# Accumulating DMAs for part of the softmax row sums, and keys loaded in two halves

## The chip, the cores and the metric

The kernel runs on one core of one Trainium2 chip. The metric is the device time of one execution in microseconds. A core has five engines that work side by side, each through its own queue, strictly in order: TensorE (PE, matrix products), VectorE (DVE), ScalarE (ACT), GpSimd (POOL) and SyncE (SP). In this kernel SP issues nearly all DMAs, and GpSimd issues those with an index list. An engine waits at the head of its queue until what its next instruction reads has been written and what it overwrites has been read; everything behind that instruction waits too.

## The reference

Two batches of 1024 tokens with 512 features go through one transformer block: attention with 16 heads of 32 features, then a mixture of experts with 8 experts and a shared one, each followed by an addition of its input and a layer norm. The part that the change touches is the attention:

```python
q = _split(lora_linear(x, Wq, bq, Bq, Aq))
k = _split(lora_linear(x, Wk, bk, Bk, Ak))
v = _split(lora_linear(x, Wv, bv, Bv, Av))
scores = jnp.einsum('bhqd,bhkd->bhqk', q, k) * SCALE
attn = jax.nn.softmax(scores, axis=-1)
out = jnp.einsum('bhqk,bhkd->bhqd', attn, v)
...
return lora_linear(out, Wo, bo, Bo, Ao)
```

All arithmetic is float32, and the kernel keeps that precision by splitting operands into a high and a low part.

## The kernel before

The kernel has three stages. The first projects q, k and v and stores them in HBM. The second, about 157 to 630 us of the profile, is the attention with its output projection. The third is the expert layer.

The attention is cut into 16 units. Unit u takes the group g = u // 2 of four heads of one batch and half u % 2 of its queries (512). A unit has eight steps, one for each block kc of 128 keys, so that step t is unit t // 8, block t % 8; there are NS = 128 steps. In step t:

- `st_step` makes, for each of the four heads, 128 keys by 512 queries of scores (st, line 604) and their exponential on ScalarE (line 613). Two heads share one tile pt of 128 x 2 x 512 floats, so a step writes two tiles, called pair 0 and pair 1. The tiles come from a pool of PTB = 13 buffers; a buffer is free again once every reader of its tile is done.
- `s1_step` runs LEAD = 12 steps ahead: four score blocks a step with queries on the partitions (s, line 183), whose row maxima VectorE takes (mt, line 191). They go through three PSUM banks. At the end of a unit `finish_max` transposes the maxima (mp) and stores them by DMA as two further rows of the queries, so that st comes out with the maximum already taken off.
- `av_step(t - 1)` multiplies the last step's exponentials with the values (av, line 634), summed over the unit's eight steps in one PSUM bank.
- `add_step` sums the exponentials of a unit's blocks (line 623): the tiles of block 0 serve as the sums, and those of blocks 1 to 6 are added to them, each with an addition of 128 x 1024 floats for each pair. Block 7 (`DIRECT`) is not added; `finish` reads it by itself. In units 0 to 13 VectorE adds pair 0 of block 1 and pair 1 of block 2 (`ON_DVE`), and GpSimd the rest; for units 14 and 15 `DVE_END` lists what VectorE adds.
- `finish(u)` lets TensorE sum the sums over the keys with a matrix of ones (sm, line 657), in step FIN = 3 of the next unit. Up to unit 13, ScalarE copies the result (rc, line 671) and two small DMAs bring the 2048 denominators onto 128 partitions; `invert(u)` in step REC = 4 takes the reciprocal of 128 x 16 elements (line 681) and spreads it again with five DMAs. From unit RDIR = 14 on VectorE takes the reciprocal of all 128 x 512 at once (line 667).
- `normalize(u)` in step 7 multiplies av with it on VectorE (line 696), copies the high part on ScalarE (698) and subtracts it on VectorE (700).

Beside them SP loads what comes next: `load_k` the keys of the next group, in three DMAs of 512 KB into one of two tiles, in step 0 of an even unit; `load_q` the queries; `load_v` the values; `load_res` blocks of the input x, to which GpSimd adds a bias three steps later (`add_res`, line 709). In units 8 to 10 the first batch's output projection is woven in (`oproj`).

In this stage every engine follows the program's order: the loop over t calls the functions, and what goes between the four heads of a step stands in the lists between[0] to between[3]. No scheduler moves anything. PSUM banks and pt buffers are chosen when the program is built; the chip only waits.

Of the kernel before, what the change touches and what calls it, by code (L numbers as in the profile page):

```python
# [36 lines left out]
OPER = 4  # L37
PTB = 13
OHB = 3
# [14 lines left out]
NO_DIR = (NU - 2,)  # L54
FIN = 3
REC = 4
XTB = 5
ON_DVE = ((1, 0), (2, 1))
EARLY = (1, 0)
OPROJ_AT = (65, 67, 69, 71, 73, 75, 77, 79)  # L60
RES_AT = tuple(8 * i + 6 for i in range(8)) + (70, 78, 86, 94, 98, 102, 106, 110)
RES_ADD = 3
RB = 2
# [4 lines left out]
MPJ, MPP = 0, 2  # L68
RDIR = NU - 2
FINE, NRME = 2, 4  # L70
DVE_END = {
    NU - 2: ((1, 0), (2, 1), (4, 1), (5, 1), (6, 0), (6, 1), (7, 0), (7, 1)),
    NU - 1: ((1, 0), (2, 0), (3, 0), (4, 0), (5, 0), (6, 0), (6, 1)),
# [20 lines left out]
def kernel(  # L94
# [47 lines left out]

    def load_k(g):
        kt = Ks[g % 2]
        for blk, hl in ((0, 0), (1, 1), (2, 0)):
            sp.dma_start(
                out=f(kt[32 * blk : 32 * blk + 32]),
                in_=qk_d[1, g // NG, g % NG, hl].rearrange("(h p) t -> p h t", p=32),
            )
# [435 lines left out]
    with ph2, tc.manual_schedule(engines={mybir.EngineType.PE}):  # L585
# [38 lines left out]

        def early(t, pr):
            return t // 8 not in DVE_END and (t % 8, pr) == EARLY

        def av_step(t):
# [4 lines left out]
            for h in range(4):  # L633
# [7 lines left out]
                )  # L641
            for pr in range(2):
                if not early(t, pr):
                    add_step(t, pr)

        def direct(u):
# [31 lines left out]
        def invert(u):  # L678
            r16 = fin[u]
            rd = dram.tile([4, 512], F32, name=f"rd{u}")  # L680
            dve.reciprocal(r16, r16)
            sp.dma_start(out=rd.rearrange("h (j c) -> (h j) c", c=16), in_=r16)
            rc = ap.tile([P, 512], F32, name=f"rb{u}", tag="rb", bufs=1)
            for h in range(4):
                sp.dma_start(
                    out=rc[32 * h : 32 * h + 32, :],
                    in_=rd[h : h + 1, :].partition_broadcast(32),
                )
            fin[u] = rc
# [56 lines left out]
        for t in range(NS):  # L746
            u, k = t // 8, t % 8
            if k == 0:
                if u % 2 == 0 and 2 <= u and u // 2 + 1 < B * NG:
                    load_k(u // 2 + 1)  # L750
                if u >= 1 and u + 2 < NU:
                    load_q(u + 2)
                if u % 2 and NG <= u // 2 + 1 < B * NG:
                    load_v(u // 2 + 1)
            if t in RES_AT:
                load_res(RES_AT.index(t))
            between = [[], [], [], []]
            if early(t, 0):
                between[2].append(lambda: add_step(t, 0))
            if t + LEAD < NS:  # L760
# [4 lines left out]
            if t:  # L765
                between[1].append(lambda: av_step(t - 1))
                if u and k == (FINE if u == NU - 1 else FIN):
                    between[1].append(lambda: finish(u - 1))
            if u:
                if k == (NRME if u == NU - 1 else 7):  # L770
                    between[0].append(lambda: normalize(u - 1, (0,)))
                    between[1].append(lambda: normalize(u - 1, (1,)))
                    between[2].append(lambda: normalize(u - 1, (2,)))
            if t - RES_ADD in RES_AT:
                between[3].append(lambda: add_res(RES_AT.index(t - RES_ADD)))
            st_step(t, between)
            if k == REC and 1 <= u < NU - 1:
                invert(u - 1)
# [9 lines left out]
            if t - NS >= OPROJ1:  # L788
                next(op10, None)
        av_step(NS - 1)  # L790
        finish(NU - 1)
        normalize(NU - 1, (0,))
# [457 lines left out]
```

## Time and profile before

| What | Value |
|---|---|
| Median of 3 runs | 1080.75 us (1079.41 to 1081.03) |
| Profiled execution, its own time | 1070.33 us |
| Its span, from the first instruction to the last | 1068.6 us |
| Mean granted TensorE clock | 0.991 |
| Busy in the span: PE, DVE, ACT, POOL | 1038.4, 747.8, 530.4, 574.7 us |
| Additions of exponentials on POOL and on DVE | 151 of 2413 ns, 43 of 2132 ns |
| Row maxima on DVE | 512 of 681 ns |
| Keys, queries, median time to landing | 6.9 us, 5.7 us |

The span is that of one execution under the profiler. Busy times are unions of an engine's instructions; TensorE's matrix products overlap and their ends are modelled, so its share tells little about short waits. A group line gives line, engine, operation, output and inputs, shapes and count, then busy time and mean, then the engine's idle time before it and what ended most of it. In answers on waits, "A <- B" is engine A waiting for B's instruction; "issue" means that nothing in the profile explains the wait. PEld is TensorE's load of weights, which comes ahead of the product that uses them. The profiled execution is some 10 us shorter than the median of the runs.

### The profile page before, as it was taken

The numbers are of one execution on the slowest core, as the hardware profiler recorded it, in microseconds if no ns is written. First come the engines' busy times: TensorE is split into PE (matmuls) and PEld (weight loads), VectorE is DVE, ScalarE is ACT, GpSimd is POOL, SyncE is SP. The second block draws the span as 40 slices with busy tenths as digits, with TensorE's granted clock in tenths as the row PEclk, the third lists the DMA queues.
The fourth block names the chain that finished last, engine by engine and source line by source line (L and its number), as shares of the span: only waits on it lengthen the run. The fifth ranks groups of instructions, "written<-read, shape, count | busy, mean of one in ns | idle before, by whom it ended". The sixth has DMA issues, their size and how long they took to land. (4 is left out here: it accounts for less than half of the span.)

```text
span 1068.6 us, 16466 instructions
## 1 busy us (share of the span) xinstructions
PE 1038.4 (97%) x5994; PEld 744.8 (70%) x5994; DVE 747.8 (70%) x1217; ACT 530.4 (50%) x1026; POOL 574.7 (54%) x379
## 2 busy tenths in 40 slices
PE   8999999999999999999999999999999999999996
PEld 6888774444444455554444358889999999999995
DVE  6732787899999987889999785333532457777762
ACT  5422214666666655556666656222322356665552
POOL 5000007888888887768998577000050026776674
PEclk9999998999999999999999999999999999999999
DMA  9866860141414242043520113000073356677731
GB/s 301 278 220 202 256 190 21 42 105 47 110 51 110 71 111 71 15 97 71 120 81 22 52 40 127 23 10 21 21 236 120 108 168 228 241 251 258 251 104 60
DMA packets 77585, 131.24 MB, mean 123 GB/s; under 512 B 14344, under 2 KB 23048, under 8 KB 77504
## 3 DMA queue, kind: packets, MB, share of 16 engines
q1 hardware_dynamic: 73664, 117.59, 37.1%
q0 software_dynamic: 3840, 12.60, 3.2%
q8 instruction: 47, 0.77, 0.3%
q14 instruction: 34, 0.28, 0.1%
HBM read 96.10 MB, written 33.80 MB: 122 GB/s over the span
## 5 line engine op out<-in xcount | busy, mean ns | idle before, releaser
L623 POOL TENSOR_TENSOR pt<-pt,pt 128x1024 f32<-128x1024 f32 x151 | 360.4, 2413 | 206.3 <-ACT pt L613 189.1
L191 DVE TENSOR_REDUCE mt<-s 128x1 f32<-128x512 f32 x512 | 323.8, 681 | 42.5 <-PE s L183 42.4
L613 ACT ACTIVATE pt<-st 128x512 f32<-128x512 f32 x512 | 270.9, 602 | 144.1 <-PE st L604 140.3
L604 PE MATMUL st<-qs,ks 98*128 98x512 f32 x512 | 216.4, 433 | 1.9 <-ACT pt L613 1.2
L183 PE MATMUL s<-ks,qs 96*128 96x512 f32 x512 | 204.1, 406 | 12.8 <-DVE mt L191 11.9
L604 PEld LDWEIGHTS st<-qs,ks 98*128 98x128 f32 x512 | 96.5, 190 | 137.3 <-issue 89.1
L864 PE MATMUL h<-xthe,w13s 128*128 128x256 f32 x704 | 129.9, 284 | 0.0
L183 PEld LDWEIGHTS s<-ks,qs 96*128 96x128 f32 x512 | 97.9, 191 | 41.4 <-DVE mt L191 26.9
L852 POOL TENSOR_TENSOR w2s<-w2r,w2s 128x512 fp32r<-128x512 f32 x42 | 65.9, 1592 | 96.9 <-ACT w2s L851 96.7
L864 PEld LDWEIGHTS h<-xthe,w13s 128*128 128x128 f32 x704 | 110.7, 191 | 0.3
L864 PE MATMUL h<-xtle,w13s 128*128 128x256 f32 x352 | 100.2, 285 | 0.0
L623 DVE TENSOR_TENSOR pt<-pt,pt 128x1024 f32<-128x1024 f32 x43 | 91.4, 2132 | 3.4 <-ACT pt L613 2.9
L634 PE MATMUL av<-pt,vt 128*32 128x512 f32 x512 | 75.0, 605 | 0.0
L634 PE MATMUL av<-pt,x1b 128*32 128x512 f32 x512 | 69.9, 619 | 0.0
L1012 POOL DMA_INDIRECT xd_d<-x1a,slot_i x8 | 8.0, 996 | 112.0 <-DVE slot_i L1009 109.9
L864 PEld LDWEIGHTS h<-xtle,w13s 128*128 128x128 f32 x352 | 67.4, 191 | 0.7
L908 PE MATMUL y<-w2s,hs 128*128 128x512 f32 x260 | 60.9, 390 | 0.0
L908 PEld LDWEIGHTS y<-w2s,hs 128*128 128x128 f32 x260 | 48.2, 188 | 10.2 <-DVE hs L890 0.5
L310 PE MATMUL o<-xl,wh 128*128 128x512 f32 x128 | 50.8, 397 | 0.9 <-POOL xl L296 0.9
L310 PE MATMUL o<-xh,wh 128*128 128x512 f32 x128 | 50.7, 396 | 0.8 <-ACT xh L295 0.8
L325 ACT ACTIVATE oh<-o,bqk_sb 128x512 fp32r<-128x512 f32 x32 | 22.0, 690 | 59.1 <-PE o L310 55.9
L310 PE MATMUL o<-xh,wl 128*128 128x512 f32 x128 | 50.5, 394 | 0.0
(822 smaller groups left out, 1760.2 us busy)
## 6 DMA issues: line engine op xcount, KB each, us to landing
qs<-qkd SPq DMA_DIRECT2D x48, 256.0 KB, 5.7
ks<-qkd SPq DMA_DIRECT2D x24, 512.0 KB, 6.9
x1a<-in_w_dram SPq DMA_DIRECT2D x24, 512.0 KB, 6.1
w2r<-in_w_dram SPq DMA_DIRECT2D x42, 256.0 KB, 2.9
qkd<-oh SPq DMA_DIRECT2D x32, 256.0 KB, 2.5
qkd<-ol SPq DMA_DIRECT2D x32, 256.0 KB, 2.5
x1b<-in_w_dram SPq DMA_DIRECT2D x16, 512.0 KB, 4.9
x1b<-in_wT_dram SPq DMA_DIRECT2D x16, 256.0 KB, 5.2
```

Source lines behind the costliest of these rows:

```text
L183: pe.matmul(s1, Qs[u % 3][0:96, h, qt * P : qt * P + P], Ks[g % 2][0:96, h, kh * 512 : kh * 512 + 512], start=True, stop=True,)
L191: dve.tensor_reduce(mts[u][:, c, kh : kh + 1], s1, AX.X, ALU.max)
L310: pe.matmul(o, lhs, rhs, start=k + i == 0, stop=k + i == KC + 1)
L325: act.activation(oh, o, AF.Identity, bias=bias)
L604: pe.matmul(sb, Ks[g % 2][:, h, kc * P : kc * P + P], Qs[u % 3][:, h, :], start=True, stop=True,)
L613: act.activation(pts[t, h // 2][:, h % 2, :], sb, AF.Exp, scale=SCALE)
L623: eng.tensor_tensor(accs[u, pr], accs[u, pr], pts[t, pr], ALU.add)
L634: pe.matmul(avs[u][32 * h : 32 * h + 32, :], vts[g][:, kc, 32 * h : 32 * h + 32], pts[t, h // 2][:, h % 2, :], start=kc == 0, stop=kc == 7 ...
L852: pool.tensor_tensor(hl[:, 1, :], raw, f(hl[:, 0, :]), ALU.subtract)
L864: pe.matmul(hp[:, j * 256 : j * 256 + 256], lhs, rhs[:, k, :], start=n == 0, stop=n == 11,)
L908: pe.matmul(o, lhs, rhs, start=n == 0, stop=n == 16)
L1012: sc_ = pool.indirect_dma_start(out=xd_d, out_offset=bass.IndirectOffsetOnAxis(ap=slot_i[:, i : i + 1], axis=0), in_=x1[i // 8][:, i % 8, ...
```

## The change

- In units 0 to 13 VectorE no longer adds exponentials. Both tiles of block 1 are added to the tiles of block 2 by DMAs that accumulate, issued by GpSimd in the place of block 2. GpSimd then adds blocks 3 and 4, block 2 (now with block 1 in it), and 5 and 6, each with both pairs: ten additions in a unit, as before. In unit 13 block 6 goes by DMA into block 7 too, and blocks 3, 4, 2 and 5 are added.
- The pool of exponentials gets 14 buffers for 13.
- `finish` moves from step 3 to step 4 of the next unit, `invert` from 4 to 5, `normalize` from step 7 to step 0 of the unit after.
- Unit 13's reciprocal is taken directly (RDIR 13 for 14).
- In unit 14 VectorE adds blocks 1 and 7 of pair 0 and blocks 1 to 7 of pair 1 (nine for eight). Its additions of blocks 1 and 2 are put behind the last maxima, in step 115.
- The keys come in two halves: columns 0 to 511 in step 6 of an odd unit, 512 to 1023 in step 0 of the next unit, two steps later.
- The last two additions of bias to x move to steps 118 and 119.

```diff
-PTB = 13
+PTB = 14
-FIN = 3
-REC = 4
+FIN, FINQ = 4, 1
+REC = 5
+NRM = 0
+K_AT = 6
-ON_DVE = ((1, 0), (2, 1))
-EARLY = (1, 0)
+ON_DVE = ()
+ON_DMA = {NU - 3: (1, 6)}
+ADDS = {0: (0,), 2: (1,), 3: (3,), 4: (4,), 5: (2,), 6: (5,), 7: (6,)}
+ADDS_END = {0: (0,), 2: (1,), 3: (3,), 4: (4,), 5: (2,), 7: (6, 5)}
-RES_ADD = 3
+RES_ADDS = tuple(t + 3 for t in RES_AT[:14]) + (118, 119)
-RDIR = NU - 2
-FINE, NRME = 2, 4
+RDIR = NU - 3
+FINE, NRME = 2, {NU - 2: 7, NU - 1: 4}
 DVE_END = {
-    NU - 2: ((1, 0), (2, 1), (4, 1), (5, 1), (6, 0), (6, 1), (7, 0), (7, 1)),
+    NU - 2: ((1, 0), (7, 0)) + tuple((i, 1) for i in range(1, 8)),
...
-    def load_k(g):
+    def load_k(g, cs=slice(0, 1024)):
         kt = Ks[g % 2]
         for blk, hl in ((0, 0), (1, 1), (2, 0)):
             sp.dma_start(
-                out=f(kt[32 * blk : 32 * blk + 32]),
-                in_=qk_d[1, g // NG, g % NG, hl].rearrange("(h p) t -> p h t", p=32),
+                out=f(kt[32 * blk : 32 * blk + 32, :, cs]),
+                in_=qk_d[1, g // NG, g % NG, hl].rearrange("(h p) t -> p h t", p=32)[:, :, cs],
             )
...
-            for pr in range(2):
-                if not early(t, pr):
+        def adds(t):
+            u, kc = t // 8, t % 8
+            if u in DVE_END:
+                for pr in range(2):
                     add_step(t, pr)
+                return
+            for j, pr in product((ADDS_END if u in ON_DMA else ADDS).get(kc, ()), range(2)):
+                i = u * 8 + j
+                if j in ON_DMA.get(u, (1,)):
+                    pool.dma_start(out=pts[i + 1, pr], in_=pts[i, pr], accum_op=ALU.add)
+                else:
+                    add_step(i, pr)
...
-                    load_k(u // 2 + 1)
+                    load_k(u // 2 + 1, slice(512, 1024))
...
+            if k == K_AT and u % 2 and u // 2 + 2 < B * NG:
+                load_k(u // 2 + 2, slice(0, 512))
...
-            if early(t, 0):
-                between[2].append(lambda: add_step(t, 0))
...
                 between[1].append(lambda: av_step(t - 1))
+                if t == NS - LEAD - 1:
+                    between[3].append(lambda: (adds(t - 2), adds(t - 1)))
+                elif t != NS - LEAD - 2:
+                    between[1].append(lambda: adds(t - 1))
                 if u and k == (FINE if u == NU - 1 else FIN):
-                    between[1].append(lambda: finish(u - 1))
+                    between[1 if u == NU - 1 else FINQ].append(lambda: finish(u - 1))
             if u:
-                if k == (NRME if u == NU - 1 else 7):
-                    between[0].append(lambda: normalize(u - 1, (0,)))
-                    between[1].append(lambda: normalize(u - 1, (1,)))
-                    between[2].append(lambda: normalize(u - 1, (2,)))
-            if t - RES_ADD in RES_AT:
-                between[3].append(lambda: add_res(RES_AT.index(t - RES_ADD)))
+                for v in [u - 2] * (k == NRM and 1 < u < NU - 1) + [u - 1] * (k == NRME.get(u)):
+                    between[0].append(lambda v=v: normalize(v, (0,)))
+                    between[1].append(lambda v=v: normalize(v, (1,)))
+                    between[2].append(lambda v=v: normalize(v, (2,)))
+            if t in RES_ADDS:
+                between[3].append(lambda: add_res(RES_ADDS.index(t)))
             st_step(t, between)
-            if k == REC and 1 <= u < NU - 1:
+            if k == REC and 1 <= u <= RDIR:
                 invert(u - 1)
...
         av_step(NS - 1)
+        adds(NS - 1)
         finish(NU - 1)
```

More of the change, by code (lines that the diff above doesn't have):

```diff
@@ L1 @@
 from contextlib import ExitStack
-from itertools import cycle
+from itertools import cycle, product
 import concourse.bass as bass
@@ L623, in add_step @@
                 eng.tensor_tensor(accs[u, pr], accs[u, pr], pts[t, pr], ALU.add)
-        def early(t, pr):
-            return t // 8 not in DVE_END and (t % 8, pr) == EARLY
         def av_step(t):
@@ L682, in invert @@
             sp.dma_start(out=rd.rearrange("h (j c) -> (h j) c", c=16), in_=r16)
-            rc = ap.tile([P, 512], F32, name=f"rb{u}", tag="rb", bufs=1)
+            rc = ap.tile([P, 512], F32, name=f"rb{u}", tag="rc", bufs=1)
             for h in range(4):
```

## The prediction

> **What bounds the kernel now.** I read the page first: its busy shares and its costliest groups.
>
> ```profile
> span 1068.6 us, 16466 instructions
> PE 1038.4 (97%) x5994; PEld 744.8 (70%) x5994; DVE 747.8 (70%) x1217; ACT 530.4 (50%) x1026; POOL 574.7 (54%) x379
> ...
> L623 POOL TENSOR_TENSOR pt<-pt,pt 128x1024 f32<-128x1024 f32 x151 | 360.4, 2413 | 206.3 <-ACT pt L613 189.1
> L191 DVE TENSOR_REDUCE mt<-s 128x1 f32<-128x512 f32 x512 | 323.8, 681 | 42.5 <-PE s L183 42.4
> ...
> L623 DVE TENSOR_TENSOR pt<-pt,pt 128x1024 f32<-128x1024 f32 x43 | 91.4, 2132 | 3.4 <-ACT pt L613 2.9
> ...
> L1012 POOL DMA_INDIRECT xd_d<-x1a,slot_i x8 | 8.0, 996 | 112.0 <-DVE slot_i L1009 109.9
> ```
>
> TensorE is nearly always busy, but that mean hides stages, and its modelled ends hide short waits. All edits lie in the attention steps, about 157 to 630 us, so next come the busy times by window, one unit of eight steps each (us, TensorE, weight loads, VectorE, ScalarE, GpSimd, clock):
>
> ```profile
> 301.00:329.00 28.00, 27.34 (x147) 13.12 (x146) 25.96 (x41) 17.96 (x37) 24.95 (x12) 1.00 0.18 49
> 422.00:462.00 40.00, 38.65 (x194) 22.05 (x195) 32.67 (x56) 21.43 (x40) 28.43 (x20) 1.00 0.19 50
> ```
>
> In an ordinary unit VectorE is at 93% and GpSimd at 89%; ScalarE has 10 us free. The second row is a unit with output projections in it: there TensorE alone has the work. Who waits for whom in that ordinary unit (us in total, times, longest):
>
> ```profile
> PEld st L604 <- issue: 5.9, 7, 0.8
> ...
> POOL pt L623 <- ACT pt L613: 1.7, 1, 1.7
> PEld s L183 <- DVE mt L191: 1.5, 2, 0.9
> POOL pt L623 <- DVE pt L623: 1.2, 1, 1.2
> ```
>
> So TensorE waits for VectorE twice in a unit. The timeline shows where, in the unit that begins at 273.6 us:
>
> ```profile
> 278.21 1.23 DVE L623 TENSOR_TENSOR pt<-pt,pt 128x1024 f32<-128x1024 f32 x1
> ...
> 280.09 0.19 PEld L183 LDWEIGHTS s<-ks,qs 96*128 96x128 f32 x1 [0.57 <-DVE mt L191]
> ...
> 284.70 3.36 DVE L623 TENSOR_TENSOR pt<-pt,pt 128x1024 f32<-128x1024 f32 x1
> ...
> 288.71 0.19 PEld L183 LDWEIGHTS s<-ks,qs 96*128 96x128 f32 x1 [0.92 <-DVE mt L191]
> ```
>
> Both stalls follow a VectorE addition: the maxima queued behind it are late, the three s banks fill, and TensorE stands. From the first exponential of one step to that of the next, the steps of that unit take 2.95, 3.34, 3.23, 4.80, 4.03, 3.25, 2.99 and 3.24 us, 27.8 together; neighbours agree within 0.1.
>
> **What the Trainium skill says.** "SBUF — State Buffer", section "Who interferes with whom": a VectorE instruction with two SBUF inputs contends with a GpSimd one that reads SBUF, and the later one blocks. The trace agrees: the addition takes 1.23 us while GpSimd waits and 3.36 us beside its additions. "DMA: Bandwidth & Descriptors", section "SWDGE vs HWDGE vs iDMA": accumulation in a DMA is for GpSimd's queue only, which writes the descriptors in software. The kernel before has no such DMA. Its section "Specifications" puts that path's start at about 1 us; the indirect DMAs here are near it, 996 ns.
>
> **The change, part by part, in an ordinary unit.**
>
> VectorE loses 1.23 + 3.36 = 4.59 us, from 25.96 to 21.4 us. The two stalls go. What is TensorE's own time? A step without a stall is 3.02 us; the row sums (sm) add 1.73 (from av at 283.59 to the next st at 286.31 it takes 2.72 us instead of 0.99); the transpose of the maxima adds 0.40 (2.47 instead of 2.07 us for four pairs). Steps 3 to 5 should then take 3 x 3.02 + 1.73 + 0.40 = 11.19 us and take 12.08; step 2 has 0.2 to 0.5 too much. So 1.3 us at most can go, to 26.5 us.
>
> GpSimd now adds pair 1 of step 1, pair 0 of step 2 and both pairs of steps 3 to 6. After the change both pairs of step 1 go by DMA into step 2's tiles, and it adds both pairs of steps 2 to 6: ten again. Ten at 2.36 (two take 4.70 to 4.75) and one residual addition of 1.1 to 1.3 are 24.9 us, as now. New are two DMA issues of d each: 24.9 + 2d. No row has d. Low end: SP's issues take 0.43 to 0.54 us, so 0.4. High end: nothing excludes that reading two operands and writing one costs twice an indirect one, so 2.0. The nearest row, eight scatters of 128 rows, has 996 ns busy, and the eight start 1.3 us apart (778.3 to 787.4). A plain copy reads no index list but has a second operand to read: I take 1.1. Then GpSimd needs 27.1 us, 0.6 more than TensorE and 0.75 less than now. Break-even with 27.85 is d = 1.48.
>
> Does GpSimd's lateness reach TensorE at once? Counted from a unit's start, the DMA can be issued at 11.3 us (av of step 2 must have read the tile), and the last addition ends at 11.3 + 2.2 + 24.9 = 38.4. The row sum needs it in step 4 of the next unit, at 26.5 + 14.2 = 40.7: the move of FIN from 3 to 4 makes that slack of 2.3 us. A lag of 0.6 a unit uses it up in four units. Behind it, exponentials of later steps wait for the same tiles (14 buffers instead of 13; the build gives the tile of step 4 that of step 6 before).
>
> The DMA itself: 512 KB, 3.2 us by the skill's fit ("Anatomy of one DMA — SWDGE (gpsimd) path": 2.0 us plus bytes over 436 GB/s), 4.4 us if the destination's bytes count too; both are estimates. Step 2's sum is added after steps 3 and 4, 9.4 us later, which hides it. Tighter: the build lets the exponential of step 5 reuse the source tile of step 1, 6.7 us after the issue starts. And REC follows FIN by 0.8 us less than now: the denominators' second transfer is issued 1.7 us after the first and landed some 1.7 us before the reciprocal; the long step moves before it. Together I charge 0.3 us a unit; without VectorE's new slack it would be up to 1.
>
> At nothing: normalize moves from step 7 to step 0 of the next unit with the same three instructions (0.69 + 0.59 + 0.68 us), its av buffer is wanted a step later, and VectorE's freed time hides it; uncovered it costs the 0.24 us that step 7 shows now. The keys' halves add three SP issues of 0.43 us per group; a whole load issued at 273.25 landed at 282.5, its first reader came after 288. SP waits for nothing long there; uncovered a late key would cost the 3 us by which it missed. The residual additions moved to steps 118 and 119 fall where GpSimd idles 9.3 us.
>
> The sum against the span of 1068.6:
> - Units 1 to 7 and 11 to 13: seven or so at 1.3 (the first four of each stretch), three at 0.75, less 0.3 each: 9.1 + 2.25 - 3.0 = 8.4 us gained.
> - Units 8 to 10, with projections: waits on VectorE of 1.0, 1.6 and 2.1 us; two thirds, 3.0. GpSimd has 8 to 12 us free there.
> - Unit 0: 4.6 us of such waits, most under a lower clock; 1.0.
> - Units 14 and 15: unit 14's first stall (0.9) goes. But after the last maxima VectorE gets three more additions (1.2 to 2.5 each) and the whole reciprocal of unit 13 (3.36 as for unit 14, instead of 0.25): 6.7 to 10.6 us more, where it idles 6.8 before sm. Taken as 1.9 lost, net 1.0 lost.
>
> 8.4 + 3.0 + 1.0 - 1.0 = 11.4 us. The span becomes 1057 us; the profiled execution took 1070.33, 1.7 more than its span, and would take 1059. The runs' median is 10.4 us above that execution; the shift is carried over: 1080.75 - 11.4 = 1069 us. Nothing after 630 us changes.
>
> **The rivals.**
> - TensorE becomes the only bound (d at most 0.8, no other waits). For it: GpSimd has 2.9 us a unit free. Then 10 x 1.3 + 4.7 + 2 less 1: 18.7 gained, 1062 us. Chance 0.17.
> - The gain is eaten: GpSimd at d = 1.4 to 1.55 takes the whole unit, or the exponential of step 5 waits about 1 us for the DMA. Only units 8 to 10 gain: 1078 to 1083, 1080 us. For it: GpSimd is already at 89%. Against: d is above every indirect DMA seen but the output's (1392). Chance 0.10.
> - Slower: an issue on GpSimd costs over 1.55 us. At d = 2.0 a unit takes 28.9, ten lose 1.05 each, the end loses 2 and units 8 to 10 gain 3: +9.5, 1090 us. From d = 1.55 it decides, in GpSimd's queue between the two stretches of additions. A DMA that lands later than 7 us does the same through the buffers. Chance 0.16.
> - My forecast, 1064 to 1076: chance 0.57.
>
> **How the numbers follow.** 0.2% of the median, 2.2 us, is about what a measurement of this kernel can tell from no change. Faster: 0.17 + 0.57 and a little of the third case, 0.76. Slower: the last case and the rest of the third, 0.17. Same: 0.07. The range leaves out the worse half of the slower case and the tail below: 1058 to 1085; the likeliest one's own is 1064 to 1076.
>
> **What would show it.** No wait of s weights on mt above 0.3 us in units 1 to 7; VectorE near 21.4 us in such a unit; 16 VectorE additions instead of 43; 30 accumulating DMAs whose issue on GpSimd is 0.9 to 1.3 us; units of 26.5 to 27.3 us. Wrong it is if GpSimd is without idle time and units take 27.8 or more, if exponentials wait for a DMA or for GpSimd, or if the last row sums come more than 3 us later after the maxima's end.

## The result and the profile after

The changed kernel takes 1074.3 us (median of 8 runs, 1071.12 to 1076.1); the kernel before, run beside it, 1080.39 us (8 runs, 1078.66 to 1081.8). The ratio is 0.9942, 95% interval 0.9929 to 0.9956: 6.1 us faster. The forecast was 1069 us and 11.4 us gained, range 1058 to 1085, so the time lies in the range and in the forecast's own part of it (1064 to 1076), with half of the gain missing.

The page of the changed kernel, its busy shares and the groups that answer to those shown of before:

```profile
span 1070.8 us, 16471 instructions
PE 1033.8 (97%) x5994; PEld 744.5 (70%) x5994; DVE 697.2 (65%) x1190; ACT 529.2 (49%) x1025; POOL 596.1 (56%) x406
...
L627 POOL TENSOR_TENSOR pt<-pt,pt 128x1024 f32<-128x1024 f32 x148 | 362.0, 2909 | 11.3 <-ACT pt L617 10.8
...
L187 PE MATMUL s<-ks,qs 96*128 96x512 f32 x512 | 200.3, 398 | 5.3 <-DMA qs<-qkd 4.2
...
L655 POOL DMA_DIRECT2D pt<-pt x30 | 27.4, 1078 | 170.5 <-PE st L608 170.5
```

The line of the s products in the kernel before:

```profile
L183 PE MATMUL s<-ks,qs 96*128 96x512 f32 x512 | 204.1, 406 | 12.8 <-DVE mt L191 11.9
```

VectorE lost 50.6 us of work, GpSimd issued 30 accumulating DMAs, and TensorE's s products, which used to wait for maxima (11.9 us), now wait for the queries (4.2 us), whose transfers stand behind the keys' in SyncE's queue. But this span is 2.2 us longer than the one shown of before, although the runs are 6.1 us faster. A second profiled execution of the kernel before, the first of the experiments, has a span of 1078.7 us. With it the spans divide like this (us; a unit lasts from its first exponential to that of the next, and the last two end with the first exponential of the last step):

| Stretch | before, shown | before, second | after |
|---|---|---|---|
| start to unit 0 | 157.1 | 158.0 | 158.4 |
| unit 0 | 32.75 | 31.16 | 25.69 |
| units 1 to 7 | 195.0 | 195.1 | 191.0 |
| units 8 to 10 | 107.6 | 107.6 | 103.6 |
| units 11 to 13 | 83.9 | 84.0 | 81.2 |
| units 14 and 15 | 47.5 | 47.6 | 52.5 |
| last exponentials at | 623.9 | 623.4 | 612.4 |
| from there to the end | 444.7 | 455.3 | 458.3 |

The last exponentials come 11.0 to 11.5 us earlier, but not where the forecast put it: unit 0 gave 5.5 to 7.1, units 1 to 13 gave 10.7 to 10.9, the end took 4.9 back, and the first unit began 0.4 to 1.3 later. The last row, whose code is the same, differs by 10.6 us between the two executions of one and the same kernel.

The windows of three units after the change: an odd one, an even one, and unit 14 (columns as before: us, TensorE, weight loads, VectorE, ScalarE, GpSimd, clock, DMA share, GB/s):

```profile
293.80:320.40 26.60, 26.60 (x147) 13.06 (x145) 21.50 (x38) 17.66 (x36) 25.78 (x14) 1.00 0.39 81
320.40:348.40 28.00, 26.79 (x146) 13.01 (x145) 21.57 (x38) 17.79 (x36) 27.65 (x15) 1.00 0.70 147
560.00:592.10 32.10, 27.10 (x135) 11.07 (x134) 30.63 (x30) 17.87 (x36) 24.53 (x11) 0.95 0.29 72
```

In the odd unit TensorE is busy throughout, and the waits of s on a maximum are gone. In the even unit it stands 1.2 us, with the DMAs busy 70% of the time. The waits of the even unit name what it stands for (mx reduces a unit's maxima to one for each query of each head):

```profile
PEld s L187 <- DVE mx L198: 1.6, 1, 1.6
PE s L187 <- DMA qs<-qkd: 1.2, 1, 1.2
```

Both belong to one and the same s, the first that reads the new keys and queries: its weights' load is put down to mx, the product itself to the queries. That the transfer is what it waited for is shown by the version with x behind the keys below, in which neither wait is left. The DMA issues on SyncE ahead of that wait show the two halves of a key load (ks), the residual block (x1a) and the queries (qs):

```profile
317.79 1.73 SPq L698 DMA_DIRECT2D rb<-rd  x4
319.62 1.32 SPq L150 DMA_DIRECT2D ks<-qkd  x3
320.98 0.43 SPq L718 DMA_DIRECT2D x1a<-in_x_dram  x1
321.51 1.32 SPq L150 DMA_DIRECT2D ks<-qkd  x3
322.88 2.33 SPq L170 DMA_DIRECT2D qs<-qkd  x3
```

"Two steps apart" is 1.9 us here: the early half stands behind the spread reciprocals (rb) in SyncE's queue, and then both halves, x and the queries fill the DMA engines until 332.4; s goes on at 333.81. In the kernel before, the transfers of the same unit filled the engines from 329.5 to 340.2 us, the last part of the queries landed at 341.37, and the first s that reads them ran at 343.30.

Unit 14 on VectorE:

```profile
573.06 5.66 DVE L627 TENSOR_TENSOR pt<-pt,pt 128x1024 f32<-128x1024 f32 x3
578.65 0.27 DVE L209 TENSOR_TENSOR ml<-mp,mh 16x128 fp32r<-16x128 f32 x1
578.85 3.18 DVE L627 TENSOR_TENSOR pt<-pt,pt 128x1024 f32<-128x1024 f32 x1
581.95 3.34 DVE L680 RECIPROCAL rc<-sm 128x512 f32<-128x512 f32 x1
```

Three additions stand ahead of ml, the low part of the last maxima. TensorE's next st needs the PSUM bank that ml reads, so it stands 2.14 us (576.8 to 579.0), runs the 3.4 us from 579.3 at half clock, and step 4 of unit 14 takes 7.7 us instead of the 5.0 of an odd unit. The late reciprocal then delays normalize, and step 7 takes 5.5 us.

### The profile page after: what moved, and what is told of

The parts are those of the page before. It is cut to its first block, busy times and chain, and to the rows that moved or that the text cites. A ratio compares the mean times of both kernels' runs of the same rounds, so it can differ in the third digit from the quotient of the medians.

```text
span 1070.8 us, 16471 instructions
## 1 busy us (share of the span) xinstructions
PE 1033.8 (97%) x5994; PEld 744.5 (70%) x5994; DVE 697.2 (65%) x1190; ACT 529.2 (49%) x1025; POOL 596.1 (56%) x406
## 3 DMA queue, kind: packets, MB, share of 16 engines
q0 software_dynamic: 8160, 28.33, 10.7%
## 5 line engine op out<-in xcount | busy, mean ns | idle before, releaser
L627 POOL TENSOR_TENSOR pt<-pt,pt 128x1024 f32<-128x1024 f32 x148 | 362.0, 2909 | 11.3 <-ACT pt L617 10.8
L608 PE MATMUL st<-qs,ks 98*128 98x512 f32 x512 | 214.1, 428 | 3.3 <-DVE ml L209 2.1
L187 PE MATMUL s<-ks,qs 96*128 96x512 f32 x512 | 200.3, 398 | 5.3 <-DMA qs<-qkd 4.2
L655 POOL DMA_DIRECT2D pt<-pt x30 | 27.4, 1078 | 170.5 <-PE st L608 170.5
L928 PEld LDWEIGHTS y<-w2s,hs 128*128 128x128 f32 x260 | 48.2, 188 | 10.2 <-DVE hs L910 0.5
L314 PE MATMUL o<-xh,wh 128*128 128x512 f32 x128 | 50.6, 395 | 1.7 <-ACT xh L299 1.0
```

Of the source, the lines that this page charges most:

```text
L187: pe.matmul(s1, Qs[u % 3][0:96, h, qt * P : qt * P + P], Ks[g % 2][0:96, h, kh * 512 : kh * 512 + 512], start=True, stop=True,)
L314: pe.matmul(o, lhs, rhs, start=k + i == 0, stop=k + i == KC + 1)
L608: pe.matmul(sb, Ks[g % 2][:, h, kc * P : kc * P + P], Qs[u % 3][:, h, :], start=True, stop=True,)
L627: eng.tensor_tensor(accs[u, pr], accs[u, pr], pts[t, pr], ALU.add)
L655: pool.dma_start(out=pts[i + 1, pr], in_=pts[i, pr], accum_op=ALU.add)
L928: pe.matmul(o, lhs, rhs, start=n == 0, stop=n == 16)
```

## The experiments

All ratios are to the kernel before, run on the same chip.

| Version | us, median | ratio, 95% interval |
|---|---|---|
| kernel before again | 1079.8 | 1.0005 (0.9992 to 1.0018) |
| before, VectorE's additions left out | 1060.08 | 0.9812 (0.9788 to 0.9836) |
| after, VectorE's additions back, no DMAs | 1116.77 | 1.0343 (1.0311 to 1.0374) |
| after, DMAs left out | 1071.09 | 0.9910 (0.9883 to 0.9938) |
| before, accumulating DMAs alone | 1118.27 | 1.0350 (1.0334 to 1.0366) |
| after, x behind the keys | 1071.85 | 0.9917 (0.9889 to 0.9945) |
| after, keys whole | 1075.46 | 0.9941 (0.9920 to 0.9961) |
| after, early half at step 5 | 1084.84 | 1.0049 (1.0031 to 1.0067) |
| after, old end of additions | 1073.32 | 0.9932 (0.9908 to 0.9956) |
| after, early half at step 5 and old end | 1088.84 | 1.0084 (1.0059 to 1.0109) |
| after, ml ahead of additions | 1074.74 | 0.9943 (0.9924 to 0.9963) |
| after, x behind the keys, unit 14 shared anew | 1070.49 | 0.9894 (0.9873 to 0.9914) |

### The kernel before once more

No edit.

> The kernel before once more, for another profiled execution of it. In its profiled execution the expert layer's 16th to 24th gated products take 24.0 us of the trace, in the changed kernel's and in every one of the experiments' so far 30.6 to 38.5 us, with TensorE at half clock for 10 us there; its median is 10 us above that execution. If the stall while the tokens are scattered is part of an ordinary execution of this program too, and the profiled one was a lucky one: this one's profile shows it (32 us or more, half clock for 10 us), and its own time is 1078 to 1082 us. If the change makes the stall: it is missing here again and the profiled time is near 1070 us. The ratio of the times is 1.00 in both cases.

The window from the 21st to the 36th gated product of the expert layer (by their activations), in the execution shown of before:

```profile
762.70:833.80 71.10, 71.10 (x505) 67.07 (x504) 24.66 (x78) 14.71 (x39) 15.65 (x16) 1.00 0.43 138
```

and in this second one:

```profile
762.10:844.00 81.90, 75.96 (x505) 69.22 (x504) 24.56 (x78) 14.72 (x40) 15.62 (x16) 0.94 0.37 120
```

The same instructions take 10.8 us more: TensorE is idle for 5.9 us of the window and at half clock for 10.2 us. The changed kernel's execution takes 82.4 us there, and every other version's profile has half clock for 10.2 or 13.7 us in this stall. So the stall belongs to ordinary executions of both kernels, and the one shown of before was without it: that is the 10 us by which it lay below the median. A second execution of before therefore compares better with after's. Why the weight loads stall there for what the trace calls issue, during the scatter of the tokens, wasn't tried.

### VectorE's additions left out of the kernel before

```diff
                 eng = dve if (kc, pr) in DVE_END.get(u, ON_DVE) else pool
+                if eng is dve and u not in DVE_END:
+                    return
...
-            act.copy(rc, sm)
+            act.activation(rc, sm, AF.Identity, bias=ones32[:, 0:1])
```

> The kernel before with VectorE's two additions a unit left out in units 0 to 13, nothing in their place: those exponentials are missing from the row sums, and 1.0 is added to the sums of units 0 to 13 as they are copied, so that no sum is zero. Theory (VectorE's additions hold back the maxima and nothing else binds): ordinary units fall from 27.85 to 26.5 us, with no wait of s weights on mt in steps 2 and 3; 15 to 18 us in all with units 8 to 10, ratio 0.983 to 0.986. Rival (GpSimd at 89% is next and sets the pace): units stay above 27.3 us, ratio above 0.992.

One of its ordinary units (columns as above):

```profile
290.80:317.50 26.70, 26.70 (x146) 13.02 (x145) 21.49 (x38) 17.87 (x36) 24.80 (x12) 1.00 0.19 52
```

27.85 us became 26.7, unit 0 took 25.68 us, no product of TensorE waits more than 1.0 us in the attention, and no stretch of it runs at half clock. The last exponentials come at 603.0 us, 20.4 us earlier than in the second execution of before, and the runs are 18.8 us faster, somewhat more than the first theory's 15 to 18. Together with the next experiment this shows the prediction's cause: the two additions, by way of the maxima, were what kept TensorE waiting. It is also about the gain that the change could have had with transfers that cost nothing and the old end: after reaches 612.4.

### VectorE's additions back in the changed kernel

```diff
-ON_DVE = ()
+ON_DVE = ((1, 0), (2, 1))
+EARLY = (1, 0)
...
-            if u in DVE_END:
-                for pr in range(2):
+            for pr in range(2):
+                if not early(t, pr):
                     add_step(t, pr)
-                return
+            return
...
+            if early(t, 0):
+                between[2].append(lambda: add_step(t, 0))
```

What follows that return, the accumulating DMAs among it, is no longer reached.

> The changed kernel with VectorE's two additions per ordinary unit put back where the kernel before has them (the pair (1,0) ahead of a maximum's pieces in step 2, the pair (2,1) after it), GpSimd adding the rest and no accumulating DMA at all; every other edit of the change stays (keys in two halves, later reciprocal and normalize, the split of the last additions). My theory, that VectorE's additions delay the maxima: the odd units go from 26.65 us back to 27.5 to 28.0 us, with waits of TensorE's s on a maximum again, and the even ones, where the late keys already cost 1.2 to 1.5 us, to 28 us or a little more; over 11 units that is 8 to 13 us, 1082 to 1088 us, a ratio to the kernel before of 1.002 to 1.008. Rival, that the other edits (the later normalize and reciprocal) made the units shorter and the DMAs did nothing: units stay within 0.3 us of the changed kernel's and the time within 3 us of 1074 us, 0.993 to 0.997.

Far slower than either expectation. Waits of units 2 to 4 on TensorE:

```profile
PE s L188 <- DVE mt L196: 6.9, 6, 1.9
```

The waits on maxima are back, in step 2 and, larger than before, in step 4: 1.9 us against 0.92. Six stretches of half clock (3.4 us each) follow such waits in the attention, a seventh the wait on ml in unit 14 that the changed kernel has too, and ordinary units take 28.1 to 33.8 us. That the sums' products, now a step later than the addition, no longer cover part of the wait is the likely reason why it grew; it is argued, not shown. Shown is that the rest of the change (the later row sums, inversions and normalizations, the halves of the keys and the end's new split) gains nothing by itself: with VectorE's additions it costs 36.6 us.

### The DMAs left out of the changed kernel

```diff
-                    pool.dma_start(out=pts[i + 1, pr], in_=pts[i, pr], accum_op=ALU.add)
+                    if u in ON_DMA:
+                        pool.dma_start(out=pts[i + 1, pr], in_=pts[i, pr], accum_op=ALU.add)
...
-            act.copy(rc, sm)
+            act.activation(rc, sm, AF.Identity, bias=ones32[:, 0:1])
```

> The changed kernel with the accumulating DMAs left out in units 0 to 12, so that block 1 of the exponentials is missing from these units' sums of rows (1.0 is added to each sum in their inversion instead, so the output is another); unit 13 keeps its four. It tells what the DMAs themselves cost. Theory, that they are free, since GpSimd has room and TensorE's own work is the bound: odd units stay at 26.6 to 26.7 us, even ones at 27.9 to 28.4 us since the keys' transfers remain late, 1072 to 1076 us, ratio 0.992 to 0.996. Rival, that their 512 KB per unit crowd the DMA engines and are what makes the keys late: even units fall by 0.7 us or more in step 4, 1067 to 1071 us, ratio 0.988 to 0.991. Rival, that issuing them holds GpSimd's additions by the recorded 2.2 us a unit and through them the sums: the waits of the sums' matmuls get shorter by 1 us or more and units of both kinds shorten.

Odd units from 3 on stay at 26.6 to 26.8 us: for them the DMAs are free. Step 4 of unit 2 falls from 6.73 to 5.21 us, that of unit 12 from 6.44 to 5.93, that of unit 6 hardly (6.45 to 6.33). So their traffic is a part of the keys' lateness and not all of it, and at most a few us in all: the interval overlaps that of the change. The attention ends 2.7 us earlier, and another 2.1 us are saved at the very end of the program, where each accumulating DMA has a price of its own (see the last part of why the prediction was right).

Their issue on GpSimd can be read in the changed kernel's timeline:

```profile
277.93 1.77 POOL L655 DMA_DIRECT2D pt<-pt  x2 [0.35 <-PE st L608]
279.08 24.05 POOL L627 TENSOR_TENSOR pt<-pt,pt 128x1024 f32<-128x1024 f32 x10
...
305.17 1.77 POOL L655 DMA_DIRECT2D pt<-pt  x2 [0.82 <-PE st L608]
```

One record lasts 1.08 us, but the pair is over in 1.15 us, when the first addition starts: each holds the queue 0.57 us. The ten additions follow at 2.35 us as before, although their records grew to 2.9 us, since they overlap. In the changed kernel they end 8.6 to 10.9 us into the next unit. GpSimd then waits for TensorE again: it is not the bound.

### The DMAs alone in the kernel before

```diff
-PTB = 13
+PTB = 14
...
-ON_DVE = ((1, 0), (2, 1))
+ON_DVE = ()
+ADDS = {0: (0,), 2: (2,), 3: (1,), 4: (4,), 5: (5,), 6: (3,), 7: (6,)}
...
+            for j, pr in product(ADDS.get(kc, ()), range(2)):
+                i = u * 8 + j
+                if j == 1:
+                    pool.dma_start(out=pts[i + 2, pr], in_=pts[i, pr], accum_op=ALU.add)
+                else:
+                    add_step(i, pr)
...
-            rc = ap.tile([P, 512], F32, name=f"rb{u}", tag="rb", bufs=1)
+            rc = ap.tile([P, 512], F32, name=f"rb{u}", tag="rc", bufs=1)
```

The 14th buffer and the one buffer that rc and rb share are in the changed kernel too.

> The kernel before with one part of the change alone: VectorE adds nothing in the ordinary units, and GpSimd's queue issues accumulating DMAs that add block 1 into block 3 instead (block 3 is added to the sum late, after block 5, so that the sums can end where they did). Keys come whole, reciprocal, normalize and the last two units' additions stay as they were. If the DMAs' part carries the whole gain and the other parts of the change cost what the odd and even units and unit 14 show (1.2 to 1.5 us in each even unit, 5 us in unit 14): units at 26.7 to 26.9 us, unit 14 at about 27 us, 1060 to 1064 us, ratio 0.981 to 0.985. If the sums now come late because GpSimd is full (10 additions of 2.35 us, the residual's 1.1 us and the issue of 1.15 us are 25.8 of 26.7 us), as I assumed when I moved the reciprocal with the rest: a wait of 1 us or more at the sums' matmuls in step 3 of each unit, units of 27.5 us or more, and 1070 us or more.

The first expectation missed by far, and the second has the time but not the cause: the kernel is 35 us slower, though no sum waits for GpSimd. The DMAs were issued on GpSimd at 264.21 and 264.8. SyncE's issues after that, in which rd stores the small reciprocals and rb can be issued only when rd has landed:

```profile
266.67 0.92 SPq L689 DMA_DIRECT2D rd<-r  x1
271.51 1.73 SPq L692 DMA_DIRECT2D rb<-rd  x4
```

SyncE's wait ahead of rb is put down to rd (3.9 us), not to the shared buffer. The windows between (the last two columns are DMA share and GB/s):

```profile
266.00:268.00 2.00, 2.00 (x13) 0.89 (x13) 1.23 (x3) 0.88 (x3) 2.00 (x2) 1.00 1.12 217
268.00:270.00 2.00, 2.00 (x14) 0.86 (x12) 2.00 (x4) 1.78 (x4) 2.00 (x2) 1.00 1.07 207
```

The accumulating pair fills all DMA engines until 271 (a share above 1 comes from packets that overlap), and a store of 8 KB lands only with its end: 4.84 us from rd to rb, 4.8 to 6.5 in the units up to 13, against 1.6 to 1.7 in most units of before. The store's 128 packets run from 269.25 to 270.97, between those of the pair; in the changed kernel they take 0.2 us (261.97 to 262.17). The Trainium skill says why this may be ("DMA: Bandwidth & Descriptors", section "Issuing engines are not separate DMA queues"): transfers of all issuing engines run on the same 16 DMA engines and interleave there. The trace agrees: those 1.7 us are spent side by side with the pair. What the delay holds up is on VectorE (four units, from 246 to 400 us):

```profile
DVE mt L191 <- PE s L183: 37.4, 40, 2.3
DVE av L703 <- DMA rb<-rd: 11.2, 4, 3.5
```

normalize waits 2 to 3.5 us for rb at the head of VectorE's queue, with the maxima behind it; TensorE follows, and half clock follows that in 11 places. In the changed kernel the pair is issued a step earlier (in flight from 252 to 258 in that unit), rd goes out at 261.13 when it has landed, and rb 1.46 us later; and normalize has another step to spare. The change's own order of DMAs with the old places of sum and normalize wasn't tried. GpSimd's additions end 8.6 to 10.9 us into the next unit in the changed kernel, and the old row sum begins 10.5 us into a unit in the version without VectorE's additions, so it might have fitted in most units; that is not shown.

### Keys: the residual block behind them

```diff
-RES_AT = tuple(8 * i + 6 for i in range(8)) + (70, 78, 86, 94, 98, 102, 106, 110)
-RES_ADDS = tuple(t + 3 for t in RES_AT[:14]) + (118, 119)
+RES_AT = tuple(8 * i + 8 for i in range(8)) + (72, 80, 88, 96, 98, 102, 106, 110)
+RES_ADDS = tuple(t + 4 for t in RES_AT[:13]) + (105, 118, 119)
```

> The changed kernel with the loads of the residual blocks (256 KB each) moved from step 6 of a unit to step 0 of the next, behind keys and queries in SyncE's queue, so that they no longer stand between the two halves of a key load; their additions move along by as much. If the even units' longer step 4 (6.4 to 6.7 us against 5.03) comes from keys that land late behind that block: step 4 of units 2, 6 and 12 falls by 0.7 to 1.2 us, 3 to 5 us in all, 1069 to 1071.5 us, ratio 0.989 to 0.992. If the block hardly matters and the second half of the keys is late because it is issued at step 0 with less lead over its reader than before: step 4 stays at 6.4 us or more and the time within 2 us of 1074 us.

Step 4 of units 2, 6 and 12 falls to 5.01, 5.12 and 5.03 us; TensorE waits for no transfer in units 1 to 7, and all ordinary units take 26.5 to 26.8 us. The attention ends at 606.4 us, 6.0 earlier than after the change. The runs show 2.4 us of it, with overlapping intervals; the rest of the program took 460.7 us in the profiled execution against 458.3, with half clock for 13.7 us in the expert layer's stall against 10.2. That the 256 KB between the halves, ahead of the queries, made them late is shown by the steps; its worth in time is known only to a few us.

### Keys: whole, and an earlier first half

```diff
-                    load_k(u // 2 + 1, slice(512, 1024))
+                    load_k(u // 2 + 1)
...
-            if k == K_AT and u % 2 and u // 2 + 2 < B * NG:
-                load_k(u // 2 + 2, slice(0, 512))
```

> The changed kernel with the keys loaded whole at step 0 of the even units, as in the kernel before, and all the rest of the change kept. If the halves are needed since shorter units leave less time between that load and its first reader: the wait for keys in step 4 of units 2, 6 and 12 grows by 0.5 to 3 us (step 4 from 6.4 to 7 to 9.5 us) and units of both kinds stay otherwise as they are: 1076 to 1084 us, ratio 0.996 to 1.003. If the halves do nothing, or their early part harms by standing in the way of the residual block and the reciprocal's small transfers: step 4 at 6.5 us or below, and 1071 to 1074.5 us, ratio 0.991 to 0.9945.

Step 4 is 5.94, 5.95 and 6.36 us in units 2, 4 and 6 (6.73, 5.64 and 6.45 with the halves) and only in unit 12, with a stretch of half clock, 8.18 instead of 6.44. The time is that of the change within the intervals. The halves, as they stand, do nothing for the time: they are issued 1.9 us apart.

```diff
-K_AT = 6
+K_AT = 5
```

> The changed kernel with the first key half issued in step 5 instead of 6, ahead of the reciprocal's DMAs in SP's queue. Theory (in the even units TensorE waits in step 4 for keys and queries that land too late): step 4 of units 2, 4, 6 and 12 falls from 6.4 us (5.6 in unit 4) to about 5.0 us, the wait of s on the DMA of qs goes, about 5 us in all; against the kernel before 0.989 to 0.990. Rival (the long step 4 is the row sum and the transposed maxima meeting in one step, whatever the keys do): the step stays at 6.4 us and the ratio at 0.994.

Step 4 fell to 5.02 to 5.08 us, as it should, and the kernel became slower. SyncE's issues in unit 5 show the price:

```profile
325.81 1.48 SPq L150 DMA_DIRECT2D ks<-qkd  x3
327.39 0.38 SPq L695 DMA_DIRECT2D rd<-r  x1
332.45 1.71 SPq L698 DMA_DIRECT2D rb<-rd  x4
```

Here the keys' half is what rd waits for, 5.06 us to rb instead of 2.8 in the same unit of the changed kernel (1.4 to 1.8 in its others); normalize waits 2.8 us for rb, TensorE's s for the maxima behind it, and six stretches of half clock fall into the attention instead of one, four of them behind such waits of s. The profiled execution is the slowest of the 13 (1095.75 us), so that it shows more of this than the median has. It is the mechanism of the experiment with the DMAs alone, made by another transfer.

### The end: three ways to share the additions

First the old list with the small inversion, none put off:

```diff
-RDIR = NU - 3
+RDIR = NU - 2
-    NU - 2: ((1, 0), (7, 0)) + tuple((i, 1) for i in range(1, 8)),
+    NU - 2: ((1, 0), (2, 1), (4, 1), (5, 1), (6, 0), (6, 1), (7, 0), (7, 1)),
...
-                if t == NS - LEAD - 1:
-                    between[3].append(lambda: (adds(t - 2), adds(t - 1)))
-                elif t != NS - LEAD - 2:
-                    between[1].append(lambda: adds(t - 1))
+                between[1].append(lambda: adds(t - 1))
```

> The changed kernel with unit 14 as before the change: VectorE's eight additions in their old places, and unit 13's denominators brought over by DMA instead of the whole reciprocal. Theory (the three additions put behind the last maxima hold back ml, the low part of the maxima, whose bank a score block needs, and then the normalization): unit 14 falls from 32.2 us to 27 to 28 us, the wait of st on ml (2.1 us) goes; 3 to 4 us in all, ratio 0.990 to 0.991. Rival (a lower TensorE clock at 579 us made that unit long): unit 14 stays over 30 us unless the clock is full there.

Unit 14 took 35.2 us: one addition of 4.25 us on VectorE, beside GpSimd's, now stands ahead of the last maxima, s waits 3.1 us, and half clock lasts 10.2 us. The kernel's time can't be told from the change's. Together with the early half at step 5:

> Both edits at once: the first key half in step 5, unit 14 as before the change. Theory: the two losses are in different units and add up, 8 to 9 us less than the changed kernel, about 1066 us where that takes 1074; ratio about 0.986. Rival (one hides the other, or the gain is lost again behind the attention): not below the better one of the two by more than 1 us.

The losses of that half stay, and unit 14 takes 34.3 us. Then ml ahead of the additions, which go to step 116:

```diff
-RDIR = NU - 3
+RDIR = NU - 2
...
-                if t == NS - LEAD - 1:
-                    between[3].append(lambda: (adds(t - 2), adds(t - 1)))
-                elif t != NS - LEAD - 2:
+                if t == NS - LEAD:
+                    between[0].append(lambda: (adds(t - 3), adds(t - 2)))
+                if t not in (NS - LEAD - 2, NS - LEAD - 1):
```

> The changed kernel with the additions of steps 113 and 114 put behind the copy of the maxima that opens unit 15's first exponentials, instead of ahead of it, and the whole reciprocal of unit 13 replaced by the small one of the other units. If unit 14's 32.15 us come from that copy, which stands in VectorE's queue behind three additions: step 4 of unit 14 falls from 7.7 us to 5.0 to 5.5 us, the half clock after it is gone, and the unit goes to 27.5 to 29.5 us: 3 to 4.5 us, 1070 to 1071.5 us, ratio 0.990 to 0.992. If VectorE simply has too many additions at this place whatever their order (as putting the old lists back in the other experiment suggests, where the stall came one step earlier), the wait moves to another step of units 14 or 15 and the time stays within 2 us of 1074 us.

Step 4 fell to 5.58 us, and step 7 rose to 10.4: unit 13's small inversion stands behind VectorE's additions at 585.2, rb lands 1.9 us after VectorE would have used it, and ScalarE waits 7.9 us for normalize. Last, a new split, on top of x behind the keys:

```diff
-    NU - 2: ((1, 0), (7, 0)) + tuple((i, 1) for i in range(1, 8)),
+    NU - 2: ((7, 0),) + tuple((i, 1) for i in range(3, 8)),
```

with GpSimd's additions of blocks 1 and 2 in the order pair 1, pair 1, pair 0, pair 0, and none put off.

> The changed kernel with the residual blocks' loads moved behind the keys (as in the experiment before that moves them alone) and with unit 14's additions shared out anew: no addition of blocks 1 and 2 on VectorE, GpSimd takes eight (pair 1 of blocks 1 and 2 first, then pair 0 of blocks 1 to 6), VectorE six (pair 1 of blocks 3 to 7, pair 0 of block 7), and none is put off. If unit 14's 32.1 us come from VectorE having too much to add between the last maxima and the reciprocal while GpSimd stands idle for 5.75 us there: nothing stands ahead of the copy of the maxima, step 4 of unit 14 falls from 7.8 us to 5.0 to 5.7 us, step 7 from 5.5 us to 2.7 to 3.5 us, the unit to 26 to 28 us, and the half clock in it is gone: 4 to 6 us below the version with the loads moved alone, 1066 to 1068 us, ratio 0.986 to 0.989. If the wait only moves, as it did in the two experiments on this place so far: unit 14 at 31 us or more and 1071 to 1074 us.

Unit 14 went to 28.0 us, as the first theory has it, but the time did not follow. TensorE in unit 15:

```profile
590.40 1.05 PE L677 MATMUL sm<-pt,ones 128*32 128x512 f32 x4 [0.35 <-DVE pt L627]
593.69 1.92 PE L677 MATMUL sm<-pt,ones 128*32 128x512 f32 x4 [2.23 <-DVE pt L627]
```

The row sums of unit 14 wait for its last additions, 6.8 us of half clock follow from 593.5, and unit 15 takes 26.0 us instead of 20.3. In three of three ways the wait moved, which suggests that the end is short of adding capacity as a whole, not only of an order. This version has the lowest median of those with the whole computation, 1070.5 us; its interval lies below that of the change, but overlaps that of x behind the keys alone, and units 14 and 15 together take 54.0 us against 52.5 after the change. So a gain from the new split is not shown.

## Why the prediction was right, and where it was not

**The cause** was right: VectorE's additions made the maxima late. The version without them, and the one with them back, show it. Most marks held: VectorE at 21.50 us in a unit (21.4 forecast), 16 additions on it, 30 DMAs. Of waits of weight loads on a maximum (mt), 1.4 us are left in unit 1, where the denominators' transfer took 4.5 us beside a pair of accumulating DMAs, and 0.8 in unit 4; the mark allowed 0.3. TensorE's own unit was put at 26.5 us from the steps' parts; the odd units from 3 on take 26.65, but the even ones up to 28.4, past the 27.3 that the mark allowed. Two signs of being wrong came in part: one exponential (at 201.97) waited 0.5 us for an accumulating DMA, and the last row sums came 42.8 us after the last maxima instead of 35.1 (2.7 us of this since the maxima end earlier in unit 14).

**GpSimd's issue, d.** Taken as 1.1 us; the record is 1.08 us, and the cost to the queue is 0.57. The step that failed is adding the record of an issue to GpSimd's unit as if the queue stood for it. With 0.57 the sum is 26.0 us, below TensorE's 26.65. The start of about 1 us that the prediction set beside that record is another thing: the first packet of the pair above starts 1.45 us after its issue (at 279.38), while GpSimd goes on. In flight the pair takes 5.15 us (to 284.53), 2.6 us a DMA, which is nearer to the estimate that counts the destination's bytes too (2.4 us of its 4.4) than to the other (1.2 of 3.2). Rival 1's mechanism, with TensorE the only bound, is what odd units show, and the 0.75 us charged as the lasting gain of three units was too little. The slower rival, whose price was d above 1.55, had no part in it.

**Units 1 to 7 and 11 to 13**: 8.4 us forecast, 6.8 measured (4.0 and 2.8). In odd units 1.2 us was gained, in unit 2 the wait for the transfers cost 0.5 us more than the gain. The step that failed is "at nothing" for the keys: it took the lead of a load over its reader, 5.5 us, from the landing of the keys. But the same s reads the new queries, which land behind the keys: at 341.37 in unit 6 and 533.43 in unit 12 of the kernel before, for an s at 343.30 and 534.30. The lead was 1.9 and 0.9 us. And the change brings that s forward, from 14.0 to 12.1 us after the unit's start where nothing is late: the stalls ahead of it are gone, and the row sum (1.73 us), which stood ahead of it in step 3, now stands behind it in step 4. That alone uses the lead up; the two accumulating DMAs of 512 KB and the residual block between the halves make up the rest. The prediction gave the price of a late key as what it missed by, and that was 1.2 to 1.5 us in units 2, 6 and 12.

**Units 8 to 10**: 3.0 forecast, 4.0 measured; two thirds of the waits was a guess on the low side.

**Unit 0**: 1.0 forecast, 5.5 to 7.1 measured. The step took the lower clock in it as given. The kernel before there:

```profile
170.51 0.40 PE L604 MATMUL st<-qs,ks 98*128 98x512 f32 x1
173.09 0.79 PE L183 MATMUL s<-ks,qs 96*128 96x512 f32 x1 [2.18 <-DVE mt L191]
```

The lower clock was a consequence: TensorE waits 2.2 us behind a VectorE addition from 170.9, half clock follows from 172.9, and in all versions without the addition both are gone from this place.

**Units 14 and 15**: 1.0 lost forecast, 4.9 measured. The cost was seen (6.7 to 10.6 us of work more for VectorE against 6.8 of room) and then taken at 1.9. What was missed is a queue: the three additions put off stand ahead of ml, and ml holds a PSUM bank that TensorE needs.

**The carrying over of the shift.** For the attention, 11.4 us forecast and 11.0 to 11.5 measured: that is luck, since the errors above cancel. The runs show 6.1. Against the second execution of before, 3.0 us are lost behind the attention (455.3 to 458.3), where the prediction has "Nothing after 630 us changes". Of these, 0.6 lie in the stall of the expert layer, whose length differs between executions (10.2 to 13.7 us of half clock). The other 2.4 lie behind the program's last DMA issue, an indexed one on GpSimd, and go with the number of accumulating DMAs:

| Versions | accumulating DMAs | from the last DMA issue to the end, us |
|---|---|---|
| before (both executions), VectorE's additions left out, VectorE's additions back | 0 | 5.9 |
| DMAs left out (unit 13 keeps its own) | 4 | 6.2 |
| accumulating DMAs alone | 28 | 8.1 |
| after, and most versions of it with all its DMAs | 30 | 8.3 |

So each accumulating DMA costs another 0.08 us at the end of the program, a price that no term of the sum had; why the end takes longer is not shown. Of the 7.8 us between the two profiled executions (1080.45 and 1072.63) the runs' medians show 6.1, since the changed kernel's profiled execution is 1.7 us faster than its median.

## What to carry to other kernels

Work moved to a DMA is paid for by the small transfers that fly beside it: look for each short chain of dependent transfers, see which engine's queue its last reader heads, and place the large transfer so that it lands before the chain starts. A shorter unit also shortens the lead of every load in it, so a transfer costed at nothing needs its lead worked out with the new steps, up to the last piece that its reader needs. And before two single traces are compared by their spans, the stretch that the change doesn't touch should be compared first.

## What the hardware showed that was not expected

- TensorE's clock halves after short waits. The Trainium skill ("TensorE: Matmul & The Clock Gate", section "🔬 Part 1: The HAM clock gate (the "warmup" mystery)") ties the half clock to an idle window of about 3.4 us that runs freely. In the attention and in the expert layer's stall, half clock lasted one, two, three or four times 3.413 us, which agrees with the window; but waits of 1.3 to 3.1 us were followed by it, less than a window, and others as long were not (in the version with VectorE's additions back, 1.9 to 2.3 us without, at 201, 259, 460 and 498 us). Three of the versions have half clock from 162 us on with no wait of TensorE's products above 0.7 us ahead of it. A wait of 2 us was followed by 3.4 us of half clock or by 10.2 (in the version with the accumulating DMAs alone); half of that, 1.7 to 5 us, is an estimate of what it costs more.
- A pair of accumulating DMAs of 512 KB each keeps all 16 DMA engines busy for 5.3 us (265.65 to 270.92 in the kernel with the DMAs alone), and a store of 8 KB issued in that time lands 3.2 us later than otherwise. On the issuing queue the pair costs 1.15 us, half of what its records say.
- Each accumulating DMA made the end of the program 0.08 us longer, 2.4 us for 30 of them, long after they had landed.
- A second execution of the kernel before held a stall of 10.8 us, with TensorE at half clock for 10.2 us, that the execution shown first didn't have.
